# A single-core transformer layer: another instruction order for the last steps, and more down projections left to the end

## The chip, the core and the metric

The kernel runs on one core of a Trainium2 chip. The metric is device time in microseconds (us) of one execution, lower is better. A core has five engines, each with its own queue that it executes in order: TensorE (PE in the profile; PEld is its weight loading), VectorE (DVE), ScalarE (ACT), GpSimd (POOL) and SyncE (SP, which here only issues DMAs). A wait in front of one instruction holds back all that is queued behind it on that engine.

## What is computed

Eight sequences of 2048 rows with 256 features, all float32. Cut to what matters:

```python
x = x + attn(layernorm(x))       # B=8, L=2048, H=256
x = x + ffn(layernorm(x))        # hidden size F=704

def attn(X):
    Q, K, V = xpos(X @ W_Q), xpos(X @ W_K, downscale=True), X @ W_V
    p = softmax(Q @ K.T)         # over all 2048 keys
    return (p * 0.9 ** abs(n - m)) @ V

def ffn(x):                      # each activation and weight is fp4-rounded
    h = silu(fp4(x) @ fp4(w_gate).T) * (fp4(x) @ fp4(w_up).T)
    return fp4(h) @ fp4(w_down).T

def fp4(t):                      # blocks of 16: scale = max|t| / 6, t/scale
    ...                          # to the nearest of 0, .5, 1, 1.5, 2, 3, 4, 6
```

## The kernel before

The 16,384 rows are 128 blocks of 128 rows; 16 blocks are one sequence. Step n of the main loop (`step`, L747; `total` is 128, `z` is 127) works on several blocks at once, as a pipeline written out by hand. The order of the calls is the order of the instructions on each engine; there is no scheduler that moves them. In step n stand:

- for block n: the scores against all 2048 keys (`scores`, L473, two halves, 8 matmul instructions each), the row maximum (`maximum`, L488, VectorE; nmax is the last of it), the exponentials with their sums (`exponentials`, L506, ScalarE), and the turning of the probabilities (`turn_p`, L527);
- for block n-1: the product with the decay factors (`decays`, L546, VectorE; only keys within 7 blocks, so 8 to 15 key blocks), the product with V (`attend`, L562), the residual and its statistics (`add_residual`, L581; a power on GpSimd, L163, gives the reciprocal deviation), the normalised xq with its fp4 scales (`normal_scales`, L596);
- for block n-2: the rounding of xq, its turning (`turn_xq`, L608, `keep_xq`, L618), gate and up with silu (`gate_up`, L628);
- for block n-3: h = silu(gate) * up (`hidden`, L650), its largest values, its normalisation and rounding (`Fp4`, L166), its turning (`turn_h`, L657);
- for block n-4: the copy of the turned h (`keep_h`, L668, ScalarE), the down projection (`down`, L679, TensorE) and the last sum with the output DMA (`finish`, L686).

Turning a tile (`turn`, L234) is a 32x32 block transpose on VectorE, a DMA to DRAM issued by ScalarE, four DMAs back issued by SP, and a copy on ScalarE. For the last blocks TensorE transposes in its place (L529, L610, L659).

`Fp4.largest` is one reduction on VectorE (L185). `Fp4.normalize` is six small VectorE operations on the scales (L192 to L197) and one wide product (L199). `Fp4.round` is three VectorE operations (L219 to L223) and three wide ones (L225 to L227). The wide ones run on GpSimd, or on VectorE where `wide_on` says so: in the main loop only for block 127.

The projections of K, Q and V of the next sequence are spread over the steps of the present one (`parts`, L90). In the last sequence there are none from step 114 on.

Three down projections, of blocks 120, 121 and 122, are `deferred` (L468): their turned h and residual wait in tiles of the K pool, so that steps 124 to 126 have no down, and they run among the last chains. In those three steps the decays and the turning of xq also come before the normalisation of h (`decays_first`, L743). After step 127 the chains of the last blocks are written out one call after another (L858 to L894).

PSUM has two pools: `ps_s` with 3 buffers for scores, gate, up and transposes, and `ps_m` with 2 buffers for attention, down and the transposes of xq.

Of the kernel before, what the change touches and what calls it, by code (L numbers as in the profile page):

```python
# [15 lines left out]
P = 128  # L16
# [18 lines left out]
def preln_xpos_retention_fp4_ffn_kernel(  # L35
# [130 lines left out]
    class Fp4:  # L166
# [34 lines left out]
        def wide(self, t):  # L201
            return t.unsqueeze(2).broadcast_to([self.rows, self.nb, QBLK])

        def round(self, wide_on=None):

            v = self.v
            big = self.big
            if big is None:
                big = ffn_p.tile([P, F], F32, tag="big", name=f"big_{self.name}")
            big = big[: self.rows, : self.n]
            nc.vector.scalar_tensor_tensor(v, v, SHRINK, v, ALU.mult, ALU.add)  # L219
            nc.vector.tensor_scalar(  # L220
                big.bitcast(I32), v.bitcast(I32), EXPONENT, None, ALU.bitwise_and
            )
            nc.vector.tensor_scalar(big, big, STEPS, STEPS, ALU.mult, ALU.max)  # L223
            wide_on = wide_on or self.wide_on
            wide_on.tensor_tensor(v, v, big, ALU.add)  # L225
            wide_on.tensor_tensor(v, v, big, ALU.subtract)  # L226
            wide_on.tensor_tensor(self.v3, self.v3, self.wide(self.scale), ALU.mult)  # L227

# [23 lines left out]
    def in_runs(t):  # L254

        return t.rearrange("p (a c i) -> p c a i", a=NSQ, i=SQ)
# [208 lines left out]

    deferred = {n: None for n in range(total - 8, total - 5)}  # L468


    raw_scores, prob = {}, {}
# [108 lines left out]

    def add_residual(n):  # L581
        if n in deferred:
            deferred[n] = act_p.tile([P, 2 * GROUP], F32, tag="kt", bufs=2 * NG, name=f"deferred_{n}")
            x1 = deferred[n][:, FC * P : FC * P + H]
        else:
            x1 = ffn_p.tile([P, H], F32, tag="x1", bufs=5, name=f"x1_{n}")
        nc.vector.scalar_tensor_tensor(
            x1, attended.pop(n), prob.pop(n), residual.pop(n), ALU.mult, ALU.add
        )
        st = small.tile([P, 6], F32, tag="st", name=f"st2_{n}")  # L590
        mv = small.tile([P, 1, 2], F32, tag="mv1", bufs=2, name=f"mv2_{n}")
        nc.vector.bn_stats(st, x1)
        nc.vector.bn_aggr(mv[:, 0, :], st)
        normal[n] = (x1, mv, layernorm_scale(mv, 1, f"f{n}"))
# [55 lines left out]
    def hidden(n):  # L650
        x1, h, up = gated.pop(n)
        h2 = h[:, :F].rearrange("p (j f) -> p j f", j=2)
        nc.vector.tensor_tensor(h2, up, h2, ALU.mult)  # L653
        hid[n] = (x1, h, Fp4(h, P, F, f"h{n}", wide_on=nc.vector if n == total - 1 else None))


    def turn_h(n):  # L657
        h = hid[n][1]
        if n >= total - 4:  # L659
            pt = ps_s.tile([P, FC + 2, P], F32, tag="s", name=f"pt_h_{n}")[:, :FC, :]  # L660
            for fc in range(FC):
                at = min(fc * P, F - P)
                nc.tensor.transpose(pt[:, fc, :], h[:, at : at + P], ident)  # L663
            keep_h(n, pt.rearrange("p c (a i) -> p c a i", a=NSQ))
        else:
            turn(h, [h[:, : (FC - 1) * P], h[:, F - P : F]], f"h{n}", "sq_h")

    def keep_h(n, src=None):  # L668
        x1, h, _ = hid[n]
        if n in deferred:  # L670
            h_t = deferred[n][:, : FC * P].rearrange("p (c q) -> p c q", c=FC)
        else:
            h_t = ffn_p.tile([P, FC, P], F32, tag="h_t", bufs=1, name=f"h_t_{n}")
        nc.scalar.copy(  # L674
            h_t.rearrange("p c (a i) -> p c a i", a=NSQ), in_runs(h) if src is None else src
        )
        hid[n] = (x1, h_t)

    def down(n):  # L679
        x1, h_t = hid.pop(n)  # L680
        pd = ps_m.tile([P, H], F32, tag="m", name=f"d_{n}")
        for fc in range(FC):
            nc.tensor.matmul(pd, h_t[:, fc, :], wd_t[:, fc, :], start=(fc == 0), stop=(fc == FC - 1))  # L683
        hid[n] = (x1, pd)
# [55 lines left out]

    kept = []

    def decays_first(n):  # L743

        return n - 4 in deferred

    def step(n):  # L747
        on = lambda d: 0 <= n - d
        k = NG + n // BPG
        turn_group = (n == 1 or n % BPG == 0 and n > 0) and k < B * NG  # L750
        load_residual(n)
        scores(n, 0)
        if on(3):
            hidden(n - 3)
        if on(2):
            mid[n - 2][2].round()
        if on(3):
            hid[n - 3][2].largest()
        maximum(n, 0)
        weights_in_step(n, "maximum")  # L760
        scores(n, 1)
        if decays_first(n):
            turn_xq(n - 2)
            decays(n - 1)
        if on(3):
            hid[n - 3][2].normalize()
        if on(4) and n - 4 < total - 4:
            keep_h(n - 4)
        if decays_first(n):
            keep_xq(n - 2)  # L770
        elif on(2):
            turn_xq(n - 2)
        if n == 2:
            keep_x(kept.pop())
        maximum(n, 1)
        exponentials(n)
        if n == 1:
            turn_p(n)
        if on(2) and n - 2 < total - 2 and not decays_first(n):
            keep_xq(n - 2)  # L780
        for g in kept:
            keep_x(g)
        kept.clear()
        weights_in_step(n, "exponentials")
        values = [(g, name) for name, g in parts(n) if name not in ROWS]
        project = lambda: [project_rotated(g, name) for name, g in parts(n) if name in ROWS]
        for g, name in values:
            project_v(g, name)
        if n != 2:
            project()  # L790
        for g, name in values:
            keep_v(g, name)
        if on(1) and n != 2 and not decays_first(n):
            decays(n - 1)
        for name, g in parts(n):
            if n == 1 and name in ROWS:
                rotate(g, name)
        if turn_group:
            if n in (1, BPG):
                statistics(k)  # L800
            normalize_on_scalar(k)
        weights_in_step(n, "decays")
        if on(3):
            hid[n - 3][2].round()
        if on(4) and n - 4 not in deferred:
            down(n - 4)
        if n == 2:
            attend(n - 1)
            weights_in_step(n, "attend")
            project()  # L810
        if n > 1 and n < total - 1:
            turn_p(n)
        for name, g in parts(n):
            if n != 1 and name in ROWS:
                rotate(g, name)
        if n > BPG and n % BPG == 1 and k + 1 < B * NG:
            statistics(k + 1)
        if n == 0:
            turn_p(n)
        if on(1) and n != 2:  # L820
            attend(n - 1)
        weights_in_step(n, "attend")
        for name, g in parts(n):
            if name in ROWS:
                load_tables()
        if on(4) and n - 4 not in deferred:
            finish(n - 4)
        if on(1):
            inverse_sum(n - 1)
        if n == total - 1:  # L830
            turn_p(n)
            down(n - 7)
            add_residual(n - 1)
            decays(n)
            inverse_sum(n)
            attend(n)
        elif on(1):
            add_residual(n - 1)
        weights_in_step(n, "residual")
        if on(3) and n < total - 1:  # L840
            turn_h(n - 3)
        if turn_group:
            turn_x(k)
            kept.append(k)
        if n == 1:
            decays(n)
        if on(1):
            normal_scales(n - 1)
        if n == total - 1:
            finish(n - 7)  # L850
        if on(2):
            gate_up(n - 2)

    for n in range(total):
        step(n)


    z = total - 1  # L858
    turn_h(z - 3)
    add_residual(z)  # L860
    mid[z - 1][2].round()
    down(z - 6)
    turn_xq(z - 1)
    normal_scales(z)
    mid[z][2].round()
    finish(z - 6)
    gate_up(z - 1)
    hidden(z - 2)
    turn_xq(z)
    hid[z - 2][2].largest()  # L870
    hid[z - 2][2].normalize()
    down(z - 3)
    hidden(z - 1)
    hid[z - 1][2].largest()
    gate_up(z)
    hid[z - 2][2].round()
    finish(z - 3)
    hid[z - 1][2].normalize()
    down(z - 5)
    hidden(z)  # L880
    hid[z][2].largest()
    finish(z - 5)
    hid[z][2].normalize()
    hid[z - 1][2].round()
    turn_h(z - 2)
    hid[z][2].round()
    down(z - 2)
    turn_h(z - 1)
    finish(z - 2)
    down(z - 1)  # L890
    turn_h(z)
    finish(z - 1)
    down(z)
    finish(z)  # L894

# [55 lines left out]
```

## Time and profile before

| what | value |
|---|---|
| median of 3 runs | 2878.14 us (2876.11 to 2879.66) |
| the profiled execution, its own time | 2880.51 us |
| its span, first to last instruction | 2878.7 us |
| VectorE busy | 2465.1 us (86%) |
| GpSimd busy | 1417.4 us (49%) |
| ScalarE busy | 1077.9 us (37%) |
| step 114 starts (first scores) | 2540.81 us |
| step 122 starts | 2704.62 us |
| step 127 starts | 2803.24 us |

Step by step in the last sequence, from the first scores of a step to those of the next, and the time that TensorE is busy in it:

| step | length, us | TensorE busy, us |
|---|---|---|
| 114 | 18.28 | 18.28 |
| 116 | 19.56 | 19.20 |
| 118 | 20.51 | 20.07 |
| 120 | 21.35 | 20.93 |
| 122 | 21.11 | 20.50 |
| 124 (no down) | 17.08 | 17.08 |
| 125 (no down) | 20.15 | 17.29 |
| 126 (no down) | 20.06 | 16.88 |

How to read it: times in the profile are us from the start of the span. A line of a timeline gives the start, the duration, the engine, the line of the kernel, the operation, what is written and read, and how many instructions were merged; a bracket gives the idle time of the engine before it and what ended that idle time. L numbers are lines of the kernel before.

### The profile page before, as it was taken

The page shows a single profiled execution, that of the slowest core. Times are in us where ns is not written, and L with a number is a line of the kernel's source. Part 1 is how long each engine was busy: PE and PEld are TensorE (multiplying, and loading weights), DVE is VectorE, ACT ScalarE, POOL GpSimd, SP SyncE. Part 2 cuts the span into 40 slices and gives each one's busy share as a digit, 9 for nine tenths or more (in the row PEclk, how much of TensorE's full clock was granted, in tenths as well). Part 3 has the DMA queues.
Part 4 walks back from the last instruction along what each step waited for, and adds up shares of the span by engine and source line. Part 5 has one row for each costly group of instructions (what it writes and reads, how often), then busy time and mean ns, then how long its engine had stood idle before and what let it go on. Part 6 is the DMA issues. An engine that isn't in the chain of part 4 may idle for free. (4 is left out here: it accounts for less than half of the span.)

```text
span 2878.7 us, 34636 instructions
## 1 busy us (share of the span) xinstructions
PE 2820.6 (98%) x9702; PEld 1835.8 (64%) x9702; DVE 2465.1 (86%) x5635; ACT 1077.9 (37%) x1665; POOL 1417.4 (49%) x1330
## 2 busy tenths in 40 slices
PE   8899999999999999999999999999999999999997
PEld 5466666666666666666666666666666666666655
DVE  7898888888888888888888888888888888888877
ACT  3243333333433434433443334343334433333331
POOL 6544545444555454554455445544555444544443
PEclk9899999999999999999999999999999999999999
DMA  5355544555455555455546554555554555345441
GB/s 189 116 159 165 170 147 139 177 174 160 143 160 167 165 158 155 150 164 170 163 143 174 163 159 149 161 154 167 156 164 149 171 167 157 116 135 153 150 124 38
DMA packets 365761, 441.97 MB, mean 154 GB/s; under 512 B 102784, under 2 KB 313088, under 8 KB 365568
## 3 DMA queue, kind: packets, MB, share of 16 engines
q1 hardware_dynamic: 307248, 263.84, 34.4%
q10 hardware_dynamic: 58320, 175.92, 16.2%
q8 instruction: 76, 1.25, 0.2%
q14 instruction: 117, 0.96, 0.1%
HBM read 246.94 MB, written 192.68 MB: 153 GB/s over the span
## 5 line engine op out<-in xcount | busy, mean ns | idle before, releaser
L479 PE MATMUL s<-kt,qt 128*128 128x512 f32 x2048 | 901.2, 592 | 4.4 <-ACT h L647 3.7
L479 PEld LDWEIGHTS s<-kt,qt 128*128 128x128 f32 x2048 | 388.3, 190 | 461.4 <-issue 422.1
L567 PE MATMUL o<-v,p_t 128*128 128x256 f32 x2944 | 659.9, 380 | 7.0 <-DVE p_t L552 7.0
L567 PEld LDWEIGHTS o<-v,p_t 128*128 128x128 f32 x2944 | 560.9, 191 | 88.3 <-DVE p_t L552 11.3
L225 POOL TENSOR_TENSOR h<-h,big_h 128x704 f32<-128x704 f32 x127 | 214.5, 1689 | 534.0 <-DVE big_h L223 533.8
L647 ACT ACT_TABLE_LOAD x126 | 161.7, 1283 | 727.5 <-DVE xq L599 472.2
L674 ACT COPY h_t<-h 128x768 f32<-128x768 f32 x121 | 100.7, 832 | 756.3 <-DMA h<-there_h 696.4
L683 PE MATMUL d<-wd_t,h_t 128*128 128x256 f32 x1500 | 350.3, 383 | 17.5 <-ACT h_t L674 16.7
L491 DVE TENSOR_REDUCE m<-s 128x1 f32<-128x1024 f32 x256 | 310.4, 1212 | 52.5 <-PE s L479 51.2
L683 PEld LDWEIGHTS d<-wd_t,h_t 128*128 128x128 f32 x1500 | 282.9, 191 | 97.3 <-ACT h_t L674 38.3
L635 PE MATMUL gate<-wg_t,xq_t 128*128 128x352 f32 x1024 | 324.4, 460 | 1.6 <-ACT xq_t L621 1.6
L635 PE MATMUL up<-wu_t,xq_t 128*128 128x352 f32 x1024 | 324.2, 459 | 0.3 <-DVE rot_k L436 0.3
L512 ACT ACTIVATE p<-s,nmax 128x1024 f32<-128x1024 f32 x256 | 283.0, 1110 | 16.5 <-DVE nmax L496 15.0
L199 POOL TENSOR_TENSOR h<-h,inv_h 128x704 f32<-128x704 f32 x127 | 176.2, 1387 | 224.8 <-DVE inv_h L197 157.1
L635 PEld LDWEIGHTS up<-wu_t,xq_t 128*128 128x128 f32 x1024 | 194.2, 190 | 109.8 <-ACT p L512 1.3
L199 POOL TENSOR_TENSOR xq<-xq,inv_x 128x256 f32<-128x256 f32 x127 | 79.0, 622 | 359.8 <-DVE inv_x L197 116.4
L635 PEld LDWEIGHTS gate<-wg_t,xq_t 128*128 128x128 f32 x1024 | 194.0, 190 | 91.6 <-ACT xq_t L621 3.6
L552 DVE TENSOR_TENSOR p_t<-runs,decay_sb 128x512 f32<-128x512 f32 (+3 forms) x414 | 239.7, 636 | 3.1 <-issue 0.4
L243 DVE STREAM_TRANSPOSE sq_p<-p 128x1024 f32<-128x1024 f32 (+7 forms) x239 | 224.2, 973 | 10.2 <-ACT p L512 10.2
L226 POOL TENSOR_TENSOR h<-h,big_h 128x704 f32<-128x704 f32 x127 | 213.8, 1683 | 10.0
L512 ACT ACT_TABLE_LOAD x125 | 160.4, 1283 | 114.0 <-DVE nmax L496 90.3
L225 POOL TENSOR_TENSOR xq<-xq,big_x 128x256 f32<-128x256 f32 x127 | 92.3, 727 | 197.2 <-DVE big_x L223 197.2
(167 smaller groups left out, 3501.8 us busy)
## 6 DMA issues: line engine op xcount, KB each, us to landing
there_h<-sq_h ACTq DMA_DIRECT2D x124, 384.0 KB, 4.5
h<-there_h SPq DMA_DIRECT2D x496, 96.0 KB, 2.3
rope_k<-in_rope_dram SPq DMA_DIRECT2D x32, 512.0 KB, 5.8
rope_q<-in_rope_dram SPq DMA_DIRECT2D x32, 512.0 KB, 6.0
xr<-in_L_attn_X_dram SPq DMA_DIRECT2D x128, 128.0 KB, 2.2
there_xq<-sq_xq ACTq DMA_DIRECT2D x126, 128.0 KB, 1.7
xq<-there_xq SPq DMA_DIRECT2D x504, 32.0 KB, 1.7
out_dram<-x SPq DMA_DIRECT2D x125, 128.0 KB, 5.3
```

The source lines that it names most:

```text
L199: self.wide_on.tensor_tensor(self.v3, self.v3, self.wide(inv), ALU.mult)
L225: wide_on.tensor_tensor(v, v, big, ALU.add)
L226: wide_on.tensor_tensor(v, v, big, ALU.subtract)
L243: nc.vector.transpose(sq[:, :, at : at + w].rearrange("p c (k i) -> p k c i", i=SQ), src.rearrange("p (k c i) -> p k c i", c=NSQ, i=SQ),)
L479: nc.tensor.matmul(ps[:, j, :], q[:, dc, ts(i % BPG, P)], kt[b, half * 2 + j][:, dc, :], start=(dc == 0), stop=(dc == 1),)
L491: nc.vector.tensor_reduce(raw_scores[n][:, half : half + 1], raw_scores[n, half], AX.XY, ALU.max)
L512: nc.scalar.activation(pr, raw_scores.pop((n, half)).rearrange("p j k -> p (j k)"), AF.Exp, bias=nmax, accum_out=sums[:, half : half + 1],)
L552: nc.vector.tensor_tensor(p_t[:, c:to, :].rearrange("p k (a i) -> p k a i", a=NSQ), pt[:, c:to], decay_sb[:, d0 + c : d0 + to, :].rearrang ...
L567: nc.tensor.matmul(po, p_t[:, j, :], vt[b, k // BPG][:, k % BPG, :], start=(j == 0), stop=(j == len(keys) - 1),)
L635: nc.tensor.matmul(ps[:, half, :FH], xq_t[:, hc, :], w[:, hc, ts(half, FH)], start=(hc == 0), stop=(hc == HC - 1),)
L647: nc.scalar.activation(h[:, :F].rearrange("p (j f) -> p j f", j=2), pss[0], AF.Silu)
L683: nc.tensor.matmul(pd, h_t[:, fc, :], wd_t[:, fc, :], start=(fc == 0), stop=(fc == FC - 1))
```

## The change

1. Steps 114 to 127 run a function of their own, `late_step`. Against `step`: the decays come right behind the first maximum and ahead of the turning of xq; the normalisation of h comes behind the second maximum; on ScalarE the copies of xq and then of h come behind the exponentials; the product with V comes ahead of down; the residual comes ahead of the last sum; `normal_scales` and `gate_up` come ahead of `turn_h`. Step 127 ends after the sum of block 126.
2. Five blocks are deferred in place of three: 118 to 122. The fifth is held in a tile of the V pool.
3. The wide operations on h of blocks 125 and 126 run on VectorE, as those of block 127 did.
4. The chains after the last step are put in another order. The five deferred downs are spread among them, and block 123's is there too.
5. The last h is rounded in two pieces and turned in two halves.

```diff
-    deferred = {n: None for n in range(total - 8, total - 5)}
+    deferred = {n: None for n in range(total - 10, total - 5)}
+    HOLD = {"tag": "kt", "bufs": 2 * NG}, {"tag": "vt", "bufs": 6}
...
-        hid[n] = (x1, h, Fp4(h, P, F, f"h{n}", wide_on=nc.vector if n == total - 1 else None))
+        hid[n] = (x1, h, Fp4(h, P, F, f"h{n}", wide_on=nc.vector if n >= total - 3 else None))
...
+    def late_step(n):
+        load_residual(n)
+        scores(n, 0)
+        hidden(n - 3)
+        mid[n - 2][2].round()
+        hid[n - 3][2].largest()
+        maximum(n, 0)
+        scores(n, 1)
+        decays(n - 1)
+        turn_xq(n - 2)
+        maximum(n, 1)
+        exponentials(n)
+        keep_xq(n - 2)
+        keep_h(n - 4)
+        hid[n - 3][2].normalize()
+        attend(n - 1)
+        inverse_sum(n - 1)
+        if n == total - 1:
+            return
+        if n - 4 not in deferred:
+            down(n - 4)
+        hid[n - 3][2].round()
+        turn_p(n)
+        add_residual(n - 1)
+        if n - 4 not in deferred:
+            finish(n - 4)
+        normal_scales(n - 1)
+        gate_up(n - 2)
+        turn_h(n - 3)
+
     for n in range(total):
-        step(n)
+        (late_step if n > total - NB + 1 else step)(n)
```

The chains behind it, as they stand now (z is 127, left is 118 to 122):

```python
turn_p(z); add_residual(z - 1); decays(z); inverse_sum(z); down(left[0])
hid[z - 3][2].round(); attend(z); finish(left[0]); normal_scales(z - 1)
down(z - 4); gate_up(z - 2); add_residual(z); turn_h(z - 3)
mid[z - 1][2].round(); finish(z - 4); down(left[1]); turn_xq(z - 1)
normal_scales(z); mid[z][2].round(); gate_up(z - 1); hidden(z - 2)
finish(left[1]); turn_xq(z); down(z - 3)
hid[z - 2][2].largest(); hid[z - 2][2].normalize(); hid[z - 2][2].round()
turn_h(z - 2); hidden(z - 1); finish(z - 3); gate_up(z)
hid[z - 1][2].largest(); hid[z - 1][2].normalize(); down(z - 2)
hid[z - 1][2].round(); turn_h(z - 1); finish(z - 2); down(left[2])
hidden(z); hid[z][2].largest(); finish(left[2]); down(left[3])
hid[z][2].normalize(); down(z - 1); finish(left[3]); down(left[4])
hid[z][2].round(pieces=...)      # the last product in two pieces
finish(z - 1); turn_h(z); finish(left[4]); down(z); finish(z)
```

More of the change, by code (lines that the diff above doesn't have):

```diff
@@ L202, in wide, with round @@
             return t.unsqueeze(2).broadcast_to([self.rows, self.nb, QBLK])
-        def round(self, wide_on=None):
+        def round(self, wide_on=None, pieces=None):
             v = self.v
@@ L226, in round @@
             wide_on.tensor_tensor(v, v, big, ALU.subtract)
-            wide_on.tensor_tensor(self.v3, self.v3, self.wide(self.scale), ALU.mult)
+            wide = self.wide(self.scale)
+            for k in pieces or [slice(0, self.nb)]:
+                wide_on.tensor_tensor(self.v3[:, k], self.v3[:, k], wide[:, k], ALU.mult)
     def turn(dst, pieces, name, tag):
@@ L582, in add_residual @@
         if n in deferred:
-            deferred[n] = act_p.tile([P, 2 * GROUP], F32, tag="kt", bufs=2 * NG, name=f"deferred_{n}")
+            hold = HOLD[n - min(deferred) >= NG]
+            deferred[n] = act_p.tile([P, 2 * GROUP], F32, name=f"deferred_{n}", **hold)
             x1 = deferred[n][:, FC * P : FC * P + H]
@@ L660, in turn_h, with keep_h @@
             pt = ps_s.tile([P, FC + 2, P], F32, tag="s", name=f"pt_h_{n}")[:, :FC, :]
[L661 to L664, printed above, removed]
+            at_once = FC // 2 if n == total - 1 else FC
+            for f in range(0, FC, at_once):
+                for fc in range(f, f + at_once):
+                    at = min(fc * P, F - P)
+                    nc.tensor.transpose(pt[:, fc, :], h[:, at : at + P], ident)
+                chunks = slice(f, f + at_once)
+                keep_h(n, pt.rearrange("p c (a i) -> p c a i", a=NSQ)[:, chunks], chunks)
         else:
             turn(h, [h[:, : (FC - 1) * P], h[:, F - P : F]], f"h{n}", "sq_h")
-    def keep_h(n, src=None):
-        x1, h, _ = hid[n]
-        if n in deferred:
+    def keep_h(n, src=None, chunks=slice(0, FC)):
+        x1, h, at = hid[n]
+        if chunks.start > 0:
+            h_t = at
+        elif n in deferred:
             h_t = deferred[n][:, : FC * P].rearrange("p (c q) -> p c q", c=FC)
@@ L674, in keep_h @@
         nc.scalar.copy(
-            h_t.rearrange("p c (a i) -> p c a i", a=NSQ), in_runs(h) if src is None else src
+            h_t[:, chunks].rearrange("p c (a i) -> p c a i", a=NSQ),
+            in_runs(h) if src is None else src,
         )
-        hid[n] = (x1, h_t)
+        hid[n] = (x1, h, h_t)
     def down(n):
-        x1, h_t = hid.pop(n)
+        x1, _, h_t = hid.pop(n)
         pd = ps_m.tile([P, H], F32, tag="m", name=f"d_{n}")
@@ L741, in preln_xpos_retention_fp4_ffn_kernel @@
     kept = []
-    def decays_first(n):
-        return n - 4 in deferred
     def step(n):
@@ L761, in step @@
         scores(n, 1)
-        if decays_first(n):
-            turn_xq(n - 2)
-            decays(n - 1)
         if on(3):
             hid[n - 3][2].normalize()
-        if on(4) and n - 4 < total - 4:
+        if on(4):
             keep_h(n - 4)
-        if decays_first(n):
-            keep_xq(n - 2)
-        elif on(2):
+        if on(2):
             turn_xq(n - 2)
@@ L778, in step @@
             turn_p(n)
-        if on(2) and n - 2 < total - 2 and not decays_first(n):
+        if on(2):
             keep_xq(n - 2)
@@ L792, in step @@
             keep_v(g, name)
-        if on(1) and n != 2 and not decays_first(n):
+        if on(1) and n != 2:
             decays(n - 1)
@@ L804, in step @@
             hid[n - 3][2].round()
-        if on(4) and n - 4 not in deferred:
+        if on(4):
             down(n - 4)
@@ L810, in step @@
             project()
-        if n > 1 and n < total - 1:
+        if n > 1:
             turn_p(n)
@@ L825, in step @@
                 load_tables()
-        if on(4) and n - 4 not in deferred:
+        if on(4):
             finish(n - 4)
@@ L829, in step @@
             inverse_sum(n - 1)
[L830 to L837, printed above, removed]
+        if on(1):
             add_residual(n - 1)
         weights_in_step(n, "residual")
-        if on(3) and n < total - 1:
+        if on(3):
             turn_h(n - 3)
@@ L848, in step @@
             normal_scales(n - 1)
-        if n == total - 1:
-            finish(n - 7)
         if on(2):
             gate_up(n - 2)
+    def late_step(n):
[27 more added lines that the diff above has]
+        turn_h(n - 3)
     for n in range(total):
-        step(n)
+        (late_step if n > total - NB + 1 else step)(n)
     z = total - 1
+    left = list(deferred)
+    turn_p(z)
+    add_residual(z - 1)
+    decays(z)
+    inverse_sum(z)
+    down(left[0])
+    hid[z - 3][2].round()
+    attend(z)
+    finish(left[0])
+    normal_scales(z - 1)
+    down(z - 4)
+    gate_up(z - 2)
+    add_residual(z)
     turn_h(z - 3)
-    add_residual(z)
     mid[z - 1][2].round()
-    down(z - 6)
+    finish(z - 4)
+    down(left[1])
     turn_xq(z - 1)
@@ L865, in preln_xpos_retention_fp4_ffn_kernel @@
     mid[z][2].round()
-    finish(z - 6)
     gate_up(z - 1)
     hidden(z - 2)
+    finish(left[1])
     turn_xq(z)
+    down(z - 3)
     hid[z - 2][2].largest()
     hid[z - 2][2].normalize()
-    down(z - 3)
+    hid[z - 2][2].round()
+    turn_h(z - 2)
     hidden(z - 1)
+    finish(z - 3)
+    gate_up(z)
     hid[z - 1][2].largest()
-    gate_up(z)
-    hid[z - 2][2].round()
-    finish(z - 3)
     hid[z - 1][2].normalize()
-    down(z - 5)
+    down(z - 2)
+    hid[z - 1][2].round()
+    turn_h(z - 1)
+    finish(z - 2)
+    down(left[2])
     hidden(z)
     hid[z][2].largest()
-    finish(z - 5)
+    finish(left[2])
+    down(left[3])
     hid[z][2].normalize()
[L884 to L889, printed above, removed]
     down(z - 1)
+    finish(left[3])
+    down(left[4])
+    hid[z][2].round(pieces=[slice(0, FC // 2 * P // QBLK), slice(FC // 2 * P // QBLK, F // QBLK)])
+    finish(z - 1)
     turn_h(z)
-    finish(z - 1)
+    finish(left[4])
     down(z)
```

## The prediction

> **What bounds the kernel now.** I read first the totals by engine, then the TensorE timeline of the last sequence, then the VectorE and GpSimd timelines of the same steps, then the waits. All times are from the profiled execution: span 2878.7 us, its own time 2880.51, the median of the runs shown 2878.14. I add the change to the median.
>
> Totals (engine, busy, share, instructions):
>
> ```profile
> PE 2820.6 (98%) x9702; PEld 1835.8 (64%) x9702; DVE 2465.1 (86%) x5635; ACT 1077.9 (37%) x1665; POOL 1417.4 (49%) x1330
> ```
>
> 98% says TensorE, but that is the mean of 128 steps. The change touches steps 114 to 127 and the end, from 2540.8 us on, so those stages are read by themselves. TensorE's waits there (us in total, times, longest):
>
> ```profile
> PE d L683 <- ACT h_t L674: 11.3, 12, 2.5
> PE pt_h L663 <- POOL h L227: 7.4, 1, 7.4
> ```
>
> Small waits in every step, and one of 7.4 us at the end. Who sets the step? VectorE in step 116 (start, us, what, idle before):
>
> ```profile
> 2577.28 1.04 DVE L243 STREAM_TRANSPOSE sq_h<-h 128x640 f32<-128x640 f32 x2 [0.97 <-POOL h L227]
> ...
> 2587.93 0.15 DVE L496 TENSOR_REDUCE nmax<-m 128x1 f32<-128x2 f32 x1
> 2588.11 1.76 DVE L552 TENSOR_TENSOR p_t<-runs,decay_sb 128x512 f32<-128x512 f32 x3
> 2589.79 0.88 DVE L219 SCALAR_TENSOR_TENSOR h<-h 128x704 f32<-128x704 f32 x1
> ...
> 2596.88 1.04 DVE L243 STREAM_TRANSPOSE sq_h<-h 128x640 f32<-128x640 f32 x2 [1.01 <-POOL h L227]
> ```
>
> and GpSimd beside it:
>
> ```profile
> 2586.62 1.39 POOL L199 TENSOR_TENSOR h<-h,inv_h 128x704 f32<-128x704 f32 x1 [1.57 <-DVE inv_h L197]
> 2591.94 1.69 POOL L225 TENSOR_TENSOR h<-h,big_h 128x704 f32<-128x704 f32 x1 [3.93 <-DVE big_h L223]
> 2593.70 1.68 POOL L226 TENSOR_TENSOR h<-h,big_h 128x704 f32<-128x704 f32 x1
> 2595.46 1.39 POOL L227 TENSOR_TENSOR h<-h,scale_h 128x704 f32<-128x704 f32 x1
> 2596.80 0.55 POOL L163 TENSOR_TENSOR rstd_f<-rstd_f,neg_half 128x1 f32<-128x1 f32 x1
> ```
>
> The reader is to see a ring: VectorE rounds h, GpSimd takes 4.94 us to finish it, VectorE's next instruction (the transpose of h) waits for that, and the rest of VectorE's step is queued behind. From one sq_h to the next is 19.60 us: 3.12 (sq_h, xq, its scales, to 2580.40), 0.39 wait for silu, 3.72 (h times up, round of x, amax, first maximum), 1.89 (scales of h), 0.31 sq_xq, 1.40 (second maximum, nmax), 1.68 (decays, 11 keys), 2.15 (round of h), 4.94 GpSimd. In these steps the ring and TensorE are about level: TensorE's steps 114 to 121 take 163.8 us (2540.81 to 2704.62).
>
> Note what is hidden: GpSimd's normalising of h (1.39, L199) lies under sq_xq, the second maximum and the decays, and the pow (L163) under sq_h.
>
> **The new order of a late step.** Three moves lengthen this ring.
>
> 1. The scales of h go behind nmax, and the round of h follows at once. GpSimd's 1.39 us plus 0.13 and 0.04 of handing over is now waited for: +1.55.
> 2. turn_h goes behind normal_scales. xq (L599) then comes first after GpSimd's round and needs the pow, which is queued behind it on GpSimd: from 2596.88 to the pow's end at 2597.35 plus 0.03, +0.50.
> 3. The decays go right behind the first maximum, ending 3.72 us after hidden starts. GpSimd's last operation on x (L227) ends 4.26 us after hidden starts (2585.05 against 2580.79). A multiplication that reads two SBUF tiles does not run beside GpSimd here: two pieces of decays that take 1.28 us elsewhere took 2.58 when they began inside a GpSimd operation. On VectorE and on GpSimd:
>
> ```profile
> 69.28 2.58 DVE L552 TENSOR_TENSOR p_t<-runs,decay_sb 128x512 f32<-128x512 f32 x2
> ```
>
> ```profile
> 68.78 1.94 POOL L227 TENSOR_TENSOR wu_rows<-wu_rows,wd_rows 128x1024 f32<-128x1024 f32 x1
> ```
>
> So +0.5 (bounds: 0 if the decays start before that operation and GpSimd yields, 0.7 with the delay of that row).
>
> Two things get shorter: silu is no longer queued on ScalarE behind the DMA of sq_h, -0.39; L192 no longer meets GpSimd's round of x (0.58 against 0.18), -0.40. And 0.1 for instructions that now begin after a wait and not overlapped. Sum with 11 keys: 19.60 + 1.55 + 0.50 + 0.50 - 0.39 - 0.40 + 0.1 = 21.5 us. Decays cost 0.148 us a key (1.68 for 11, 2.29 for 15).
>
> TensorE's own new path: the copy of h_t stands behind the exponentials on ScalarE, so down follows nmax by 5.2 (exponentials and sums to 3.9, xq_t 0.4, h_t 0.83). Then down 2.70, gate and up 4.73, scores 7.1, maximum and nmax 1.4: 21.1 us. With down left out, gate follows nmax by 4.4 and the path is 17.6. Both are below the ring, so **the ring sets every late step**, and the two further downs that leave steps 122 and 123 buy nothing there.
>
> nmax of step 114 stays at 2549.3 (the second maximum waits for scores that do not move). The 13 intervals to nmax of 127 attend to 159 keys, 12.2 on average: 13 x (21.5 + 0.148 x 1.2) = 281.5. Before, nmax of 127 ends at 2815.33, 266.0 later. **Late steps: +15.5 us.** Bounds: the 0.5 of the decays from 0 to 0.7 (-6.5 to +2.6), and 0.15 a step of rounding (2 us).
>
> The moved DMAs: h's transpose leaves VectorE later, but h_t is wanted later too. sq_h to h_t took 8.7 us (2577.28 to 2585.99), and now has about 13. xq took 5.1 to 6.0 from sq_xq to xq_t and now has 5.4 before ScalarE is free, so up to 0.6 may be waited for on TensorE's path, which has that much to spare. On SP the order of a step is the same but for turn_h after the output, and nothing there is late.
>
> **The end**, counted from nmax of 127 (63.4 us before: 2815.33 to 2878.7). TensorE's 7.40 us wait goes, and with it the cold clock behind it:
>
> ```profile
> 2863.52 1.54 PE L663 MATMUL pt_h<-ident,h 128*128 128x128 f32 x6 [7.40 <-POOL h L227]
> 2866.01 5.07 PE L683 MATMUL d<-wd_t,h_t 128*128 128x256 f32 x12 [0.94 <-ACT h_t L674]
> 2870.91 0.82 PE L663 MATMUL pt_h<-ident,h 128*128 128x128 f32 x6
> 2872.67 2.86 PE L683 MATMUL d<-wd_t,h_t 128*128 128x256 f32 x12 [0.94 <-ACT h_t L674]
> ```
>
> (5.07 us for a down against 2.86.) But two downs (2 x 2.6) come in, and VectorE becomes the bound, as h of 125 and 126 is now wholly its own. Its chain: scales of h124, residual of 126, decays of 127, round of h124 to 8.1; normal_scales of 126 beside GpSimd's three operations, each of which holds a small VectorE operation as in 2845.68 (1.61 for 0.18), to 13.8; residual of 127, rounds of x, normal_scales of 127 to 22.2. Then h125: up 0.9, finish 0.4, amax 0.9, scales 1.55, six wide or long operations 0.9 + 0.9 + 0.55 + 0.55 + 3 x 0.92 = 5.65, sum 9.4, to 31.6. h126 the same, to 41.0. h127: finish 0.4, up and amax 1.8, a wait for a left-over down to 44.3, finish 0.4, scales and product 2.5, finish 0.4, round to 52.5; finish of 126 to 52.9. TensorE fills these with the left-over downs, waiting 1.7 and 1.4 us in front of two transposes. Last: the second half of h_t to 53.5, the rest of down to 55.7, finish 56.2, and 2.7 from the last addition to the span's end as before: 58.9. **End: -4.5 us** (-7 if GpSimd holds nothing up, -2 if small operations stretch). The last product in two pieces costs a second instruction's start, below 0.1, and lets the first three transposes begin 0.4 earlier.
>
> Total +15.5 - 4.5 = +11.0: 2878.1 + 11.0 = 2889.
>
> **A rule against this change.** TensorE now stands still 2.5 to 3.1 us at a time in front of down or gate (attending ends 1.6 to 3.3 us after nmax, down starts at 5.2, gate at 4.4 to 4.7). The rows show full clock after 2.45 us of idleness (the down of step 127 took 2.86) and a cold one after 7.40, nothing between. The Trainium skill, TensorE: Matmul & The Clock Gate, "Why this matters for your kernels", advises no idle gaps over about 3 us, as a window of idleness halves the clock; by that rule the late steps stand at the edge. If each step restarted cold at the row's price, 5.07 - 2.86 = 2.2 us, TensorE's path would be 23.3 and the late steps some 22 us longer than I sum; by the rows that I have the price is 0, and I take 0.
>
> **The rivals.**
> - *TensorE's path decides (faster).* The place is the ring's GpSimd waits; if the decays and transposes that now stand around them gave enough cover, the ring would fall under 21.1 with a down and 17.6 without. nmax of 127 would come at 2549.3 + 8 x 21.1 + 5 x 17.6 = 2806.1, 9.2 earlier; with the end -13.7: 2864. For it: steps 125 and 126 take 20.1 and visibly wait for silu. Against: VectorE executes in order, and its order in the changed kernel has nothing between the scales and the round of h but one 0.14 us reciprocal. Chance 0.06.
> - *No hold on the decays and a clean end (no change).* 15.5 - 6.5 - 7 and some slack: +2, 2880. Against: the row at 69.28. Chance 0.09.
> - *The clock falls in the late steps (slower still).* 2889 + 22 = 2911. Chance 0.04.
> - *The change does not do what it says*: the tiles for the two further deferred blocks could be late. They follow K and V tiles of the sixth sequence, last read before step 114, so I give this nothing.
>
> **The numbers.** The forecast, 0.81: 2889, by itself from 2884 to 2896 (decays 0.3 to 0.7, end -2 to -6). The range reaches to 2881 for the no-change case. About 0.2% (5.8 us) is what a measurement of this kernel can tell from no change: slower 0.85, same 0.09, faster 0.06.
>
> **What would show it.** Right: sq_h to sq_h 21.2 to 22.1 us in steps 115 to 126, with and without a down; h L219 waiting for GpSimd's L199 in each; xq waiting for the pow; the first piece of decays near 1.1 us where 0.64 is normal; TensorE idle in front of down and gate; nmax of 127 near 2831; the end 59 us after it with no wait over 2 us on TensorE. Wrong: steps without a down shorter by 2 us or more than those with one, a late step under 20.5 us, or clock under 1.00 before 2830.

## The result, and the profile after

The changed kernel takes 2891.76 us (median of 5 runs, 2890.40 to 2895.08), the kernel before on the same chip 2878.14 (5 runs, 2876.11 to 2883.19). The ratio is 1.0045, 95% interval 1.0034 to 1.0056: slower by 13.6 us, where 11 were predicted. The profiled execution took 2890.82 us, its span is 2888.9.

Totals of the changed kernel (engine, busy, share, instructions). VectorE's 2465.6 us were 2465.1 before, TensorE and ScalarE are within 2 us of before, and GpSimd has 13.3 us less, as the wide operations on two blocks have left it. The loss is nothing that a total can show:

```profile
PE 2822.1 (98%) x9702; PEld 1839.4 (64%) x9702; DVE 2465.6 (85%) x5644; ACT 1076.2 (37%) x1666; POOL 1404.1 (49%) x1322
```

Cut where the prediction cut it, at the end of nmax of steps 114 and 127 (us, profiled executions):

| | before | predicted | after |
|---|---|---|---|
| late steps, nmax of 114 to nmax of 127 | 266.0 | 281.5 | 282.6 |
| the end, from there to the span's end | 63.4 | 58.9 | 59.5 |

What lies ahead of nmax of 114, which the change does not touch, is 2.5 us shorter in the one profiled execution (2549.3 and 2546.8); over all the runs below that stretch wanders between 2543 and 2551, so the two stages are compared by themselves.

VectorE of the changed kernel from nmax of step 116 to the decays of step 117 (start, us, what, idle before and what ended it):

```profile
2590.45 0.16 DVE L499 TENSOR_REDUCE nmax<-m 128x1 f32<-128x2 f32 x1
...
2593.65 0.89 DVE L219 SCALAR_TENSOR_TENSOR h<-h 128x704 f32<-128x704 f32 x1 [1.54 <-POOL h L199]
...
2601.25 0.41 DVE L603 TENSOR_SCALAR xq<-x,mv,rstd_f 128x256 f32<-128x256 f32 x1 [2.22 <-POOL rstd_f L163]
...
2603.37 0.97 DVE L245 STREAM_TRANSPOSE sq_h<-h 128x640 f32<-128x640 f32 x2
...
2607.94 2.28 DVE L555 TENSOR_TENSOR p_t<-runs,decay_sb 128x512 f32<-128x512 f32 x3
```

and GpSimd beside L219 and L603:

```profile
2592.23 1.39 POOL L199 TENSOR_TENSOR h<-h,inv_h 128x704 f32<-128x704 f32 x1 [4.89 <-DVE rs L580]
2595.81 1.68 POOL L225 TENSOR_TENSOR h<-h,big_h 128x704 f32<-128x704 f32 x1 [2.19 <-DVE big_h L223]
2597.57 1.67 POOL L226 TENSOR_TENSOR h<-h,big_h 128x704 f32<-128x704 f32 x1
2599.32 1.39 POOL L229 TENSOR_TENSOR h<-h,scale_h 128x704 f32<-128x704 f32 x1
2600.66 0.55 POOL L163 TENSOR_TENSOR rstd_f<-rstd_f,neg_half 128x1 f32<-128x1 f32 x1
```

GpSimd does what it did before, in the same durations. What is new is the bracket on L219: VectorE now stands for L199. The bracket on L603 stands where the transpose of h waited for L227 before (1.01 us in step 116). Now VectorE waits for the pow as well: from the start of L225 on GpSimd to VectorE's next instruction behind it are 5.44 us, where they were 4.94. VectorE's two longest waits over the late steps and the end, from 2541 us on (us in total, times, longest), show that nearly every step has them:

```profile
DVE xq L603 <- POOL rstd_f L163: 25.5, 12, 3.0
DVE h L219 <- POOL h L199: 19.9, 13, 1.5
```

TensorE's waits in the same stretch: more in front of down than before (15.1 against 11.3 us, in fewer waits), and nothing of the 7.4 us at the end:

```profile
PE d L693 <- ACT h_t L683: 15.1, 8, 3.0
PE o L570 <- DVE p_t L555: 10.7, 5, 2.3
PE gate L639 <- ACT xq_t L625: 5.0, 5, 2.3
PE pt_h L669 <- DVE h L229: 2.9, 2, 1.7
```

### The profile page after: what moved, and what is told of

Its sections match the earlier page's. It is cut to its first block, busy times and chain, and to the rows that moved or that the text cites. A ratio compares the mean times of both kernels' runs of the same rounds, so it can differ in the third digit from the quotient of the medians.

```text
span 2888.9 us, 34558 instructions
## 1 busy us (share of the span) xinstructions
PE 2822.1 (98%) x9702; PEld 1839.4 (64%) x9702; DVE 2465.6 (85%) x5644; ACT 1076.2 (37%) x1666; POOL 1404.1 (49%) x1322
## 5 line engine op out<-in xcount | busy, mean ns | idle before, releaser
L225 POOL TENSOR_TENSOR h<-h,big_h 128x704 f32<-128x704 f32 x125 | 210.7, 1686 | 503.3 <-DVE big_h L223 503.2
L693 PE MATMUL d<-wd_t,h_t 128*128 128x256 f32 x1476 | 344.2, 383 | 20.7 <-ACT h_t L683 20.3
L199 POOL TENSOR_TENSOR h<-h,inv_h 128x704 f32<-128x704 f32 x125 | 173.4, 1387 | 260.2 <-DVE inv_h L197 130.6
L199 POOL TENSOR_TENSOR xq<-xq,inv_x 128x256 f32<-128x256 f32 x127 | 79.0, 622 | 349.7 <-DVE inv_x L197 136.8
L226 POOL TENSOR_TENSOR h<-h,big_h 128x704 f32<-128x704 f32 x125 | 210.2, 1681 | 9.8
L225 POOL TENSOR_TENSOR xq<-xq,big_x 128x256 f32<-128x256 f32 x127 | 92.3, 727 | 204.9 <-DVE big_x L223 204.9
```

Of the source, the lines that this page charges most:

```text
L199: self.wide_on.tensor_tensor(self.v3, self.v3, self.wide(inv), ALU.mult)
```

## The experiments

The theory on record is the ring: VectorE and GpSimd set every late step, TensorE only follows. The rivals: TensorE's own path sets it (the late copy of h_t, or a clock that falls in the new waits); or the loss is in the new end. "Late" and "end" are the two stages of the table above; they come from one profiled execution of each kernel, the ratio from all its runs. The expectations give times in us on the scale of the first measurement (before 2878, after 2891.8); the kernel before took 2878.6 to 2883.4 us beside the experiments, so their totals are compared by the ratio.

| kernel | ratio to before on its chip, 95% interval | late, us | end, us |
|---|---|---|---|
| before | 1 | 266.0 | 63.4 |
| after | 1.0045 (1.0034 to 1.0056) | 282.6 | 59.5 |
| scales of h early | 1.0077 (1.0060 to 1.0094) | 289.4 | 59.6 |
| turn of h first | 1.0039 (1.0024 to 1.0054) | 283.2 | 59.8 |
| copy of h_t early | 1.0029 (1.0019 to 1.0039) | 278.9 | 59.6 |
| old steps, new end | 0.9983 (0.9974 to 0.9993) | 266.5 | 60.0 |
| scales and copy early | 1.0001 (0.9992 to 1.0010) | 268.9 | 59.6 |
| all three | 0.9993 (0.9984 to 1.0003) | 267.3 | 60.5 |
| three deferred | 1.0057 (1.0042 to 1.0072) | 283.7 | 62.5 |
| h on GpSimd at the end | 1.0062 (1.0045 to 1.0078) | 285.2 | 62.5 |
| xq turned first | one run: 2888.86 against 2878.87 us | 280.9 | 60.0 |
| old steps, silu first | 0.9975 (0.9965 to 0.9986) | 263.6 | 59.5 |

### Old steps, new end

The order of `step` is kept until step 126; only the end, and the five deferred downs, are new. (What `step` needs for deferred blocks, `decays_first` among it, stands in it as before; with five of them it holds in steps 122 to 126.)

```diff
-        (late_step if n > total - NB + 1 else step)(n)
+        (late_step if n == total - 1 else step)(n)
```

> The changed kernel with the steps of before in place of late_step in 114 to 126 (step 127 stays late_step); five blocks deferred, h of 125 and 126 on VectorE and the new end stay. Theory: the late steps take their 266 us again (nmax of 114 to nmax of 127; the two further downs left out buy nothing there, since steps 122 and 123 then run at the 20.1 us of 125 and 126), and the end keeps its gain of 4 us: 2874 to 2875 us, faster than before. Rival (the new end gains only because TensorE has work left over from slow steps): 2878 or more.

Late 266.5 and end 60.0: the steps are as long as before, and the end keeps its gain. The whole loss is the order of the late steps; the new end by itself gains 3.3 us here. The rival that the end loses is out.

### The copy of h_t early

```diff
         maximum(n, 1)
+        keep_h(n - 4)
         exponentials(n)
         keep_xq(n - 2)
-        keep_h(n - 4)
```

> The changed kernel with ScalarE's copy of the turned h ahead of the exponentials again, all else as changed. It takes 3 to 4 us out of TensorE's path (down no longer stands behind the exponentials) and leaves the ring. Theory (ring): TensorE stops waiting for h_t, but the steps only lose what they had above the ring, 5 us in all (the two with a cold clock, 22.7 and 23.4, come down to 21.0 and 21.5), none in the steps without a down: 2887 us. Rival (TensorE's path sets the steps with a down): 2 us and more in each of eight steps, 2875 or less.

This takes h_t off TensorE's path and leaves the ring alone. TensorE's wait in front of down is gone from the view of waits (it was the first line above); from 2541 us on it begins:

```profile
PE o L570 <- DVE p_t L555: 20.3, 13, 2.4
PE gate L639 <- ACT xq_t L625: 10.9, 9, 2.5
```

The late steps became 3.7 us shorter, and TensorE's idleness moved to the product with V and to gate. From nmax to nmax ("to 115" is from that of 114 to that of 115), with the key blocks that the decays of that step take (10, 11, 12, 13, 14, 15, 15, 14, 13, 12, 11, 10, 9). The down of a step follows its nmax, so the intervals to 115 to 122 hold a down, and the five from there on hold none:

| | to 115 | 116 | 117 | 118 | 119 | 120 | 121 | 122 | 123 | 124 | 125 | 126 | 127 |
|---|---|---|---|---|---|---|---|---|---|---|---|---|---|
| after | 22.67 | 21.18 | 21.26 | 23.86 | 21.62 | 22.59 | 21.87 | 21.81 | 21.49 | 21.27 | 21.14 | 21.00 | 20.87 |
| h_t early | 21.01 | 21.15 | 21.26 | 21.47 | 21.61 | 21.73 | 23.34 | 21.60 | 21.48 | 21.28 | 21.13 | 20.99 | 20.88 |

The lower row depends on the keys alone, the interval to 121 apart: 10 keys take 21.01 with a down (to 115) and 20.99 without (to 126), 13 take 21.47 and 21.48. That is the ring, and TensorE's path does not appear in it. The five intervals without a down are the same in both rows to 0.02 us, as expected. Without the excess of step 121 the row sums to 277.3. Against it, the changed kernel is longer in three intervals (to 115, 118 and 120), by 1.66, 2.39 and 0.86 us, which the copy of h_t cost. I expected 5 us back, and 1.6 of them went to step 121, where the decays waited 1.88 us for the DMA that brings the turned probabilities.

### The scales of h early

```diff
         turn_xq(n - 2)
+        hid[n - 3][2].normalize()
         maximum(n, 1)
...
-        hid[n - 3][2].normalize()
```

> The changed kernel with one call moved: the scales of h and its product on GpSimd come ahead of the second maximum again. Theory (the ring of VectorE and GpSimd sets the late steps): GpSimd's 1.39 us lies under the second maximum, so the ring shortens by 1.4 us; the five steps without a down get all of it (21.0 to 21.8 becomes 19.6 to 20.4, 7 us together), the steps with a down come to TensorE's path of 21.1 and more and gain 2 to 3 us together. 2882 us against the changed kernel's 2891.8, and h L219 no longer waits 1.5 us for GpSimd. Rival (TensorE's path over down sets them): the ring has slack, 2890 or more.

The expectation failed: slower than the change, 1.0077. The wait in front of L219 went as expected (in VectorE's timeline of this kernel, step 115):

```profile
2572.66 0.89 DVE L219 SCALAR_TENSOR_TENSOR h<-h 128x704 f32<-128x704 f32 x1 [0.22 <-POOL h L199]
```

and the intervals to 123 to 127, without a down, took 20.91, 20.63, 19.80, 20.35 and 20.23, 0.6 to 1.3 less than in the changed kernel. But those with a down took 22.6 to 24.15. The 1.57 us of scales now stand ahead of nmax, and nmax starts TensorE's path, on which h_t follows it. That path was level with the ring (21.1 summed); now it is 22.7, and the three such intervals whose down was not slowed took 22.60 to 22.73. VectorE waits for TensorE (waits of this kernel, first line), 28.3 us where the changed kernel has 8.8:

```profile
DVE x L699 <- PE d L693: 28.3, 9, 4.1
```

and the longer pauses of TensorE cool its clock, which is to say that the matmuls behind them take longer: downs after 3.80 and 2.39 us of idleness take 4.25 and 4.41 us, one after 2.10 takes 2.86. Five of the eight downs are cold, and their intervals are the ones of 23.4 to 24.15:

```profile
2554.07 4.25 PE L693 MATMUL d<-wd_t,h_t 128*128 128x256 f32 x12 [3.80 <-ACT h_t L683]
...
2649.32 4.41 PE L693 MATMUL d<-wd_t,h_t 128*128 128x256 f32 x12 [2.39 <-ACT h_t L683]
2673.47 2.86 PE L693 MATMUL d<-wd_t,h_t 128*128 128x256 f32 x12 [2.10 <-ACT h_t L683]
```

### Scales and copy early, and all three

The two edits above together; then with the next one too. If the ring and the copy explain both results, the two together must give the L199 term back.

> The changed kernel with both moves of e1 and e3: the scales of h ahead of the second maximum, ScalarE's copy of h ahead of the exponentials. e1 alone was slower, since the scales delay nmax by 1.6 us and so TensorE's path over h_t (13.9 us from nmax to the next scores with a cold clock, then 9.5 to nmax). Theory now (two rings that were level, VectorE with GpSimd at 21.2 and TensorE's path over down at 21.1): with the copy out of the way only the first is left, at 21.28 - 1.57 - 1.2 + 1.57 = 20.1 us for 12 keys, and TensorE's own 20.5 to 20.9 where 14 or 15 keys are attended to. nmax of 114 to nmax of 127 262 to 264 us (282.6 changed, 266.0 before), the end 59.6: 0.997 of before. Rival (the scales in front of nmax hurt by themselves): 275 us or more for the late steps, slower than before.

> e5 and also e2's move (VectorE's transpose of h ahead of normal_scales, its DMAs behind silu). Theory: another 0.4 us off the ring of VectorE and GpSimd where TensorE isn't full: late steps 259 to 262 us, the end 59.6, 0.996 of before. Rival (the ring no longer counts once TensorE's path is short): the same as e5.

With two, the first five steps took 19.68, 19.81, 19.95, 20.16 and 20.28, within 0.15 of what was expected, against 21.01 to 21.61 with the copy alone: the term that was summed at 1.55 measures 1.31 to 1.34, as 0.22 of its wait is left. But the expectation for the stage failed: the late steps came to 268.9 and not to 262 to 264, because something else is late next, in two places. In steps 120 and 121 (22.00 and 23.44) the decays wait for the DMA of the turned probabilities, 1.5 and 3.3 us (VectorE of this kernel):

```profile
2687.59 2.37 DVE L555 TENSOR_TENSOR p_t<-runs,decay_sb 128x512 f32<-128x512 f32 x4 [3.32 <-DMA runs<-there_p]
```

and the last six (20.95 to 20.23) are each 0.5 to 0.7 over what the ring would give. In the last four of them gate waits 1.9 to 2.9 us for xq_t, each time into a cold clock (4.33 us for the 8 matmuls, where 2.63 is normal behind a wait), and VectorE's first maximum then waits 0.70 for the scores (the first of the four gates):

```profile
2739.26 4.33 PE L639 MATMUL gate<-wg_t,xq_t 128*128 128x352 f32 x8 [2.91 <-ACT xq_t L625]
```

All three give 267.3, where 259 to 262 were expected, and a total that can't be told from before (0.9993, 0.9984 to 1.0003). Here the decays wait for the DMA of the turned probabilities in seven of the steps, 8.9 us together. The structure of the late step can be mended up to the old one's time; nothing here took it below.

### The turn of h first

`turn` is split: the transpose of h goes ahead of `normal_scales`, so the pow is hidden again; its DMAs stay behind silu on ScalarE.

```diff
+        transfers = turn_h(n - 3, later=True)
         normal_scales(n - 1)
         gate_up(n - 2)
-        turn_h(n - 3)
+        transfers()
```

> The changed kernel with only the VectorE part of turning h moved ahead of normal_scales; its DMAs stay behind silu on ScalarE. Theory (ring): the transpose covers GpSimd's pow again, 0.5 us a step, all of it in the five steps without a down (2.5 us) and part of it in the others: 2886 to 2889 us. Rival (TensorE's path): 2891 or more.

The intervals to 123 to 127, without a down, fell by 0.33 to 0.36 (21.13, 20.92, 20.79, 20.65, 20.54): that is what the term summed at 0.50 measures. In those with a down it bought nothing that lasted: 21.0 to 24.5, late 283.2. The total can't be told from the changed kernel's (1.0039 against 1.0045, and the intervals overlap), so the gain that was expected did not come. As with the scales, a shorter ring by itself shows only where TensorE's path is shorter still.

### Xq turned first

```diff
-        decays(n - 1)
         turn_xq(n - 2)
+        decays(n - 1)
         maximum(n, 1)
```

> The changed kernel with the turning of xq ahead of the decays in a late step (they are the other way round there). It tells what the 0.5 us are that the first piece of the decays lost beside GpSimd's last operation on x. Theory (one waits for GpSimd either way): the transpose of xq waits those 0.5 us for its operand, the decays then run alone, their first piece at 0.64 us instead of 1.15, and the ring stays at 21.0 to 21.8 us, within 0.1. Rival (the two engines lose time to each other beyond the operation that is waited for): the ring falls by 0.3 us or more.

The decays now begin after GpSimd's last operation on xq, because the transpose of xq waits for it:

```profile
2802.69 0.45 DVE L245 STREAM_TRANSPOSE sq_xq<-xq 128x256 f32<-128x256 f32 x1 [0.47 <-POOL xq L229]
2803.05 1.59 DVE L555 TENSOR_TENSOR p_t<-runs,decay_sb 128x512 f32<-128x512 f32 x3
```

The same decays took 2.01 us in the changed kernel, 0.42 more. But the wait costs 0.47, and the intervals to 123 to 127 are 21.65, 21.43, 21.30, 21.15 and 21.03, 0.15 longer than after (within 0.1 was expected). So the hold (first piece 1.08 us where 0.64 is normal) is real, and to avoid it gains the ring nothing: the transpose needs that operation of GpSimd either way. The stage is 1.7 us shorter than after all the same, on TensorE's path: with xq turned earlier ScalarE never waits for the DMA of xq_t (four waits in the changed kernel, 3.4 us), the intervals to 118 and 120 take 21.65 and 21.92 where they took 23.86 and 22.59, and one down is cold where two were.

### Three deferred, and h on GpSimd at the end

```diff
-    deferred = {n: None for n in range(total - 10, total - 5)}
+    deferred = {n: None for n in range(total - 8, total - 5)}
```

> The changed kernel with three blocks deferred, 120 to 122, as before; steps 122 and 123 have their down again and the end has two downs less. Theory (the ring sets the late steps whether a down is in them or not, and VectorE sets the end): late steps 282 to 285 us (282.6 changed; up to 2 us more where a wait for h_t lets the clock fall), end 59 to 59.6: 2891 to 2894 us. Rival (leaving the two downs out is worth their 2.6 us each): 2896 or more; or (they cost in the end what they take there): 2887 or less.

(With them the two downs `left[3]` and `left[4]` go from the chains at the end.) From sq_h to sq_h, steps 122 and 123 with their downs take 21.60 and 21.69, without them 21.81 and 21.47: the prediction's "buy nothing there" holds. But the end is 62.5 and not 59.5, which I had not expected. TensorE has nothing to do ahead of the last transposes, and the last down runs cold (TensorE, end of this kernel):

```profile
2879.16 0.63 PE L669 MATMUL pt_h<-ident,h 128*128 128x128 f32 x3 [4.93 <-DVE h L229]
...
2881.11 5.30 PE L693 MATMUL d<-wd_t,h_t 128*128 128x256 f32 x12
```

In the changed kernel two left-over downs fill that place, and the last down takes 2.76. The 2.54 between the two, and 0.46 in the transposes ahead of it, are the 3.0 us:

```profile
2878.92 2.75 PE L693 MATMUL d<-wd_t,deferred 128*128 128x256 f32 x12
...
2883.16 2.76 PE L693 MATMUL d<-wd_t,h_t 128*128 128x256 f32 x12
```

The other part of the end, h of blocks 125 and 126 on VectorE, undone:

```diff
-        hid[n] = (x1, h, Fp4(h, P, F, f"h{n}", wide_on=nc.vector if n >= total - 3 else None))
+        hid[n] = (x1, h, Fp4(h, P, F, f"h{n}", wide_on=nc.vector if n == total - 1 else None))
```

> The changed kernel with the wide operations on h of blocks 125 and 126 on GpSimd again; the order of the end is the changed one. Theory (VectorE is the end's bound and GpSimd needs 6.3 us for what takes VectorE 3.6): the late steps stay at 282.6, the end grows from 59.5 by 2.7 for each block less what VectorE does meanwhile, to 63 to 65: 2895 to 2897 us. Rival (the end's gain is its order and the left-over downs alone): the end stays at 60, 2892.

The end is 62.5, a little less than expected: a transpose waits 4.50 us for GpSimd, and what follows is cold. This part is worth 3.0 us, as much as the two downs. The two together can't be worth 6.0, since the whole end gained 3.9: without either, the other no longer helps as much.

### Old steps, silu first

The old order and the new end, and from step 114 on the DMAs of the turned h are issued behind silu (the split of `turn` above, with VectorE's order left alone). This keeps the one term of the ring that the change won, 0.39 us a step.

> e4 (the steps of before with the new end) with one thing of the new order: in steps 114 to 126 ScalarE issues the DMA of the turned h behind silu, VectorE's order is that of before. Theory: the ring of before held 0.39 us of VectorE waiting for a silu that stood behind that DMA, and in the steps without a down scores waited 1.2 us for the same silu; both go. Late steps 266.5 to 262 or 264 us, the end 60: 0.9965 to 0.998 of before, against 0.9983 for e4. Rival (the later landing of h is waited for by down, since h_t stood level with it: 0.4 to 0.7 us in each step before): the same as e4 or slower.

Late 263.6, end 59.5, ratio 0.9975 (0.9965 to 0.9986): 7 us faster than before and the lowest ratio of all these kernels, though its interval overlaps that of the old steps with the new end (0.9974 to 0.9993). The late steps gain 0.19 us a step against before, not 0.39.

## Why the prediction was right, step by step

- **The ring sets the late steps: shown for ten of the thirteen, not for "every" one.** The copy experiment made the steps depend on nothing but the number of keys, with or without a down, and in the changed kernel all but three intervals agree with its row to about 0.2 us (the one to 121 with that row's wait for the DMA taken off). From sq_h to sq_h in steps 122 to 126 the changed kernel takes 21.81, 21.47, 21.27, 21.15 and 21.00; the sum for 14 to 10 keys gives 21.94, 21.80, 21.65, 21.50 and 21.35. So the sum is 0.13 to 0.38 too long a step: 277.3 by the ring's own row against 281.5. (The prediction's own formula, 13 x (21.5 + 0.148 x 1.2), comes to 281.8; 281.5 is a slip of 0.3.) Of the twelve intervals from sq_h to sq_h six lie in the 21.2 to 22.1 that were named, three just under it (21.15, 21.15, 21.00) and three over it (22.71, 23.37, 22.58), of which more below.
- **The terms.** L199 in the open: the wait is 1.53, and to hide it again gave 1.31 to 1.34 (1.55 predicted). The pow: 0.33 to 0.36 (0.50). The hold on the decays: 0.42 to 0.44 on the instruction (0.50), though nothing is won without it. L192 takes the 0.18 that was summed. Silu freed from the DMA: in the steps that the ring sets VectorE no longer waits for it, as summed (0.39); moved alone, in the old steps, it gave 0.19. The three terms that lengthen the ring came out at or under what was summed.
- **The step that failed: "by the rows that I have the price is 0, and I take 0"**, and with it "both are below the ring". The clock does fall in the new pauses, now and then. On TensorE of the changed kernel, the down of four steps:

```profile
2551.84 4.30 PE L693 MATMUL d<-wd_t,h_t 128*128 128x256 f32 x12 [2.65 <-ACT h_t L683]
2574.52 2.86 PE L693 MATMUL d<-wd_t,h_t 128*128 128x256 f32 x12 [2.22 <-ACT h_t L683]
...
2618.30 4.35 PE L693 MATMUL d<-wd_t,h_t 128*128 128x256 f32 x12 [2.95 <-ACT h_t L683]
...
2663.74 2.86 PE L693 MATMUL d<-wd_t,h_t 128*128 128x256 f32 x12 [2.42 <-ACT h_t L683]
```

  The cold ones cost 1.4 to 1.5 us, and stand in the intervals to 115 and 118, which are 1.66 and 2.39 over the ring. That the clock is the cause in the first is seen in "xq turned first", where the same down after the same pause stayed warm and the interval took 21.17 instead of 22.67:

```profile
2551.14 2.86 PE L693 MATMUL d<-wd_t,h_t 128*128 128x256 f32 x12 [2.65 <-ACT h_t L683]
```

  The granted clock of the changed kernel from 2615 to 2622 us (stretch, its length, five engines' busy time, clock, DMA share, GB/s) is 0.76:

```profile
2615.00:2622.00 7.00, 4.05 (x12) 3.07 (x11) 4.88 (x9) 1.99 (x5) 4.76 (x4) 0.76 0.37 138
```

  The rest of what is over the ring has another cause: in the intervals to 118 and 120 the copy of xq_t waits 1.2 us for its DMA, and the copy of h_t, and so down, stands behind it. In the second of them no clock falls, and it is 0.86 us over the ring. In "xq turned first" both waits are gone, and both intervals stand 0.2 over the ring's row. On ScalarE in the second:

```profile
2662.55 0.40 ACT L625 COPY xq_t<-xq 128x256 f32<-128x256 f32 x1 [1.19 <-DMA xq<-there_xq]
```

  The prediction allowed up to 0.6 for this and gave the path "that much to spare". By the ring as it measures (21.0 to 21.7 with a down), a path of 21.1 has none to 0.6 to spare. The three intervals cost 4.9 us that were priced at 0, and the ring was summed 4.2 too long: **that the total of the late steps was right to 1.1 us is luck, since two errors cancelled.**
- **The clock at 22 us (0.04): wrong in size.** It was not each step, and by the prediction's own path only the eight steps with a down could have lengthened (17.6 + 2.2 without one stays below the ring). Paid were two downs, and two products with V in steps without a down (7.13 and 6.70 us, where 5.34 and 4.91 are normal), which cost nothing there, since those steps have slack on TensorE. The signs on record are mixed here: "clock under 1.00 before 2830" was named as a sign against, and came.
- **The end: right.** 59.5 against 58.9, with waits of 1.68 and 1.26 in front of two transposes (1.7 and 1.4 summed). VectorE's chain holds link by link: the h of 125, 126 and 127 begin 22.1, 31.5 and 41.2 us after the end of nmax of 127, where 22.2, 31.6 and 41.0 were summed:

```profile
2851.50 0.88 DVE L657 TENSOR_TENSOR h<-up,h 128x704 f32<-128x704 f32 x1
...
2860.86 0.88 DVE L657 TENSOR_TENSOR h<-up,h 128x704 f32<-128x704 f32 x1
...
2870.57 0.88 DVE L657 TENSOR_TENSOR h<-up,h 128x704 f32<-128x704 f32 x1
```

  What the prediction said of the downs there was short: the two further downs were priced as work, 2 x 2.6 us. They are also what keeps the clock up ahead of the last down, and without them the end is 3.0 longer.
- **"Two further downs buy nothing there": right** for steps 122 and 123, by the experiment, and wrong as a judgment of the part.
- **The late transfers: missed as a next limit.** The prediction found "nothing late" on SP. That holds for the long steps. As soon as they are shortened, the DMA of the turned probabilities ends VectorE's wait, most of all in the steps with 15 keys (1.5 to 3.3 us). Why it is late was not tried and stays open.

## What to carry to other kernels

Where two engines hand a tile back and forth, write down the ring with its small instructions, and ask of each move which operation of the partner it uncovers: 1.4 us of GpSimd work came into the open because six scale operations were put behind a reduction. When two paths are within 0.1 us of each other, a move that shortens one by putting its work on the other lengthens the whole, as with the scales; change both at once, and expect the third to show. Work that is left over for the end is worth something as a filler that keeps the clock up ahead of the last work: look there before it is priced as a cost.

## What the runs showed of the hardware that I had not expected

- A pause of TensorE needs less than I thought to cool it, and the length does not decide alone. From nmax of 114 on, in all twelve kernels, no matmuls ran cold without a pause of at least 1.89 us shortly before them, and after one of 2.75 us or more they always did. Between the two both occur: cold after 1.89 (gate in "scales and copy early", 4.33 us where 2.63 is normal) and 1.93 (a down in "h on GpSimd at the end", 4.54 us where 2.86 is), warm after 2.65 (a down, 2.86) and 2.74 (a product with V in "xq turned first", 5.02 us for 22 matmuls). After 2.25 us the changed kernel alone has both (products with V of 7.13 and 4.58 us, which take 5.34 and 4.48 without a pause).
- The Trainium skill, TensorE: Matmul & The Clock Gate, Part 1 ("What's actually happening"), lets the clock fall after at least one idle window of about 3.4 us, and says that the window runs free of the kernel, so that the moment of a change depends on where in it the work lands. That pauses of one length go either way in these traces would fit such a window, which no run shows; that a whole window must be idle does not agree with them, since pauses of 1.89 to 3.24 us were enough.
- The hold on VectorE by GpSimd falls on small operations too: beside GpSimd's wide ones, in the normal_scales of block 126 in the changed kernel, L603 took 1.72 us where 0.41 is usual, L192 1.15 against 0.17.
